# An RWKV block on one core: intra-chunk pair products in 64-token instead of 32-token blocks, k^T v of two chunks issued together, and a planner that counts shape changes and table loads

## The chip, the cores and the metric

The kernel runs on one core of one Trainium2 chip. The metric is device time in microseconds, as a median of several runs. A core has five engines that matter here: TensorE (PE) multiplies matrices; VectorE (DVE), ScalarE (ACT) and GpSimd (POOL) work elementwise; SyncE (SP) issues transfers. They run side by side, each through its own queue in order, and meet by semaphores. SBUF is the on-chip memory; PSUM is where TensorE writes its products.

## The reference

The input `x` is (2 sequences, 4096 tokens, 256 channels), all float32. It goes through a normalisation modulated by a condition, two RWKV layers, a second modulated normalisation and a feed-forward network with FP4 rounding. What matters here is the recurrence `_wkv` in each layer's time mix, with 4 heads of 64 channels:

```python
def step(state, inp):
    rt, kt, vt, wt = inp
    kv = kt[..., :, None] * vt[..., None, :]
    out = jnp.einsum('bhk,bhkv->bhv', rt, state + u[None, :, :, None] * kv)
    return (state * wt[..., None] + kv, out)
...
x = x + _time_mix(_ln(x, p['ln1_w']), p)
x = x + _channel_mix(_ln(x, p['ln2_w']), p)
```

`w` is a decay per channel and token. Within a chunk of tokens the recurrence can be written as products of pairs: token t receives from token s < t the value `v_s`, weighted by the sum over channels of `r_t * k_s * (decays between s and t)`; token t itself enters with the bonus `u`.

## The kernel before

Tokens go in tiles of 256 (`TT`), each two chunks of 128 (`C` = 2). A head pair fills 128 channels, so there are `J` = 2 pairs, and inside a pair `p` = 0, 1 selects the head. There are 16 tiles per sequence, hence 64 calls of `wkv` (2 sequences, 2 layers, 16 tiles).

**Order of the work.** The kernel writes generators ("streams"): a first-layer and a second-layer stream for each sequence, one for the feed-forward network, one that prepares its weights and one for the conditioning. The streams don't issue instructions themselves; they record them with `Plan`. Successive TensorE calls of one generator step form one `Op`. `Plan.run` is a list scheduler: it estimates for every recorded operation when it could start, from `weight` (the cost of an instruction), the free time of its engine and the ends of what it depends on (`after`), takes the operation that could start earliest, and emits it (`give_out`), which moves its engine's time on. So each engine's order is fixed when the kernel is built, by these estimates, and at run time each engine follows its order and waits on semaphores. All instructions recorded this way appear in the profile under one line, L248, where `give_out` calls them; they are told apart by the names of their tiles. Work tiles come from a stock of `SLOTS` = 36 tiles of 128 x 514 floats; a stream records no further while the stock is below its `least`.

**Inside `wkv`.** One call at a time holds `head_lock`. The pair weights of a chunk are built by levels l = 0 to 6. Level l handles pairs of tokens (s, t) whose highest differing bit is bit l. For l < 5 (`NLEV`) the kernel multiplies whole diagonal blocks of 32 tokens, four per chunk, `K[.., s0:s0+32]` against `R[.., s0:s0+32]`, for both chunks, both head pairs and both heads: 32 `matmul` calls of 64 rows x 32 columns with 32 moving columns. They go to `pa`, two PSUM banks (one for each head), at one of four column positions (`l % 4`). Level 5 multiplies the off-diagonal 32 x 32 blocks (two a chunk, 16 calls), level 6 the off-diagonal 64 x 64 block (one a chunk, 8 calls). After each level DVE multiplies the decays of that level into `r` and `k` (`upd`) and forms the products of decays (`nt`); the next level's products need `upd`.

Of a level's block only the entries of that level are valid. `copy_predicated` on DVE copies them with `masks[:, l]` from `pa` into `diag`; this is recorded after level 3 for levels 0 to 3, and after level 6 for level 4. Levels 5 and 6 are copied by ACT straight from `pa` into `attn` (128 x 128 pair weights per head, pair and chunk). Four ACT copies then move the 32-token blocks from `diag` to the diagonal of `attn`. Meanwhile `k` is transposed to `kt`.

Then, for each chunk: the outputs `po` = `r` S + `attn` v, then k^T v into `kv` (4 calls of 128 x 64), then on DVE the state update S = S * tot + kv. Chunk 1's outputs need the S that chunk 0 updated.

**The costs.** `weight` gives a TensorE call with up to 32 columns 19 ns, a transpose 110 ns, other calls (4n/2.4 + 6) ns, times 0.55 where two halves of the array can work side by side. Nothing is charged when TensorE's operand shape changes, nor when ACT loads another function table.

Of the kernel before, what the change touches and what calls it, by code (L numbers as in the profile page):

```python
# [8 lines left out]
F32 = mybir.dt.float32  # L9
BF16 = mybir.dt.bfloat16  # L10
I32 = mybir.dt.int32
AF = mybir.ActivationFunctionType
# [19 lines left out]
LEAST = (8, 5, 3)  # L32
RUSH = 1.0
SOON = 40.0
SLOTS = 36
STAGGER = (12, 60)
SLOTS2 = 4
TINY = 24
# [51 lines left out]


class Op:
    __slots__ = ("eng", "calls", "cost", "port", "wait", "ready", "next", "end", "banks", "tiles", "age", "late")

    def __init__(self, eng, age):
        self.eng, self.age = eng, age
        self.calls, self.banks, self.tiles, self.next = [], {}, set(), []
        self.cost = self.ready = self.end = 0.0
        self.port = False
        self.wait = 0  # L100


class Plan:
# [15 lines left out]
    SEEN = {"tensor": 55.0, "gpsimd": 80.0}  # L119
    SAME = {"vector": 34.0, "scalar": 25.0, "gpsimd": 80.0}  # L120

    def after(self, o, op):
        return o.end + (self.SAME.get(o.eng, 0.0) if o.eng == op.eng else self.LAT[o.eng] + self.SEEN.get(op.eng, 35.0))

    def __init__(self, nc, banks):
        self.nc, self.banks = nc, [(0.0, b) for b in banks]
        self.probe = banks[0]
        self.seen = {}
        self.held = {}
        self.free = {e: 0.0 for e in self.ENG}  # L130
        self.lock = {"vector": 0.0, "gpsimd": 0.0}
        self.cur = None
        self.count = 0
        for e in self.ENG:
            setattr(self, e, Recorder(self, e))
# [67 lines left out]
    def record(self, eng, fn, a, k):  # L203
        st = self.cur
        outs = [k["out"]] if "out" in k else [a[0]]
        ins = list(a[0 if "out" in k else 1:]) + [v for n, v in k.items() if n != "out"]
        ins = [v for v in ins if isinstance(v, (bass.AP, Later))]
        cost, port = weight(eng, fn, outs[0], ins)
        op = st.last if eng == "tensor" else None
        if op is None or op.next is None:  # L210
            self.count += 1
            op = Op(eng, self.count)
            op.late = st.late
            st.queue.append(op)
        st.last = op if eng == "tensor" else None
        op.calls.append((getattr(getattr(self.nc, eng), fn), a, k))
        op.cost += cost
        op.port = op.port or port
        for v in ins:
            if not is_dram(v):  # L220
                self.need(op, v, False)
        for v in outs:
            if not is_dram(v):
                self.need(op, v, True)

    def start(self, op, st):
# [7 lines left out]
            t = max(t, self.lock["gpsimd" if op.eng == "vector" else "vector"] - 100.0)  # L234
        return t

    def give_out(self, op, t):
        for b in op.banks:
            if b.real is None:
# [6 lines left out]

        for fn, a, k in op.calls:
            fn(*[real(v) for v in a], **{n: real(v) for n, v in k.items()})  # L248
        op.end = t + op.cost
        self.free[op.eng] = t + (60.0 if op.eng == "sync" else op.cost - self.LAP.get(op.eng, 0.0))  # L250
        if op.port:
            self.lock[op.eng] = op.end
        for b in op.banks:
# [62 lines left out]
        return lambda *a, **k: self.plan.record(self.eng, fn, a, k)  # L316


def is_dram(v):
    return isinstance(v, bass.AP) and v.name.endswith("_dram")  # L320


def weight(eng, fn, out, ins):
# [4 lines left out]

    n = max(v.free_size() for v in [out] + ins)
    if eng == "tensor":  # L330
        if fn == "transpose":
            return 110.0, False
        n = out.free_size()
        if n <= 32:
            return 19.0, False
        pair = (n == 64 and out.shape[0] == 64) or (ins[0].shape[0] <= 64 and out.shape[0] == P and n == TT)
        return (4 * n / 2.4 + 6) * (0.55 if pair else 1.0), False
    if eng == "sync":
        return 100.0, False
    wide = [v for v in ins if v.free_size() > 1]  # L340
# [17 lines left out]
def rwkv_adaln_fp4_kernel(ctx: ExitStack, tc: tile.TileContext, a: dict, out: bass.AP):  # L358
# [28 lines left out]

    masks = const.tile([P, NLEV, 32], I32, name="masks")  # L390
    with tc.tile_pool(name="mk", bufs=1) as mk:
        s_i = mk.tile([P, 32], I32, name="s_i")
        t_i = mk.tile([P, 32], I32, name="t_i")
        x_i = mk.tile([P, 32], I32, name="x_i")
        g_i = mk.tile([P, 32], I32, name="g_i")
        y_i = mk.tile([P, 32], I32, name="y_i")
        nc.gpsimd.iota(s_i, pattern=[[0, 32]], base=0, channel_multiplier=1)
        nc.gpsimd.iota(t_i, pattern=[[1, 32]], base=0, channel_multiplier=0)
        nc.vector.tensor_scalar(s_i, s_i, 31, None, ALU.bitwise_and)
# [190 lines left out]
    for i in range(L):  # L590
        for b in range(B):
            nc.gpsimd.memset(state[i][b], 0.0)
            for m in range(2):
                nc.gpsimd.memset(carry[i][b][m], 0.0)
    diag = keep.tile([P, 2, C, J, 32], F32, name="diag")
    attn = keep.tile([P, 2, C, J, P], F32, name="attn")
    nc.gpsimd.memset(diag, 0.0)
    nc.vector.memset(kv, 0.0)
# [143 lines left out]
    def wkv(i, b, rk_s, dec_s, v_s):  # L742
# [20 lines left out]
        for l in range(7):  # L763
            h = 1 << l
            R, K = (r0, k0) if l == 0 else (r, k)
            wid = 64 if l == 6 else 32
            col0 = (l % 4) * C * J * 32
            cols = slice(col0, col0 + C * J * wid)
            pv = pa[:, :, cols].rearrange("p a (c j t) -> p a c j t", c=C, j=J)

            if l < NLEV:
                at0 = [(q, q) for q in (0, 32, 64, 96)]
            else:
                at0 = [(0, 32), (64, 96)] if l == 5 else [(0, 64)]
            for c in range(C):
# [21 lines left out]
            pl.vector.tensor_tensor(nt, tv[:, :, 0], tv[:, :, 1], ALU.mult)  # L797
            tot = nt

            ready = {3: range(0, 4), 6: range(4, 7)}.get(l, ())  # L800
            for m in ready:
                mw = 64 if m == 6 else 32
                c0 = (m % 4) * C * J * 32
                mc = slice(c0, c0 + C * J * mw)
                if m < NLEV:
                    pl.vector.copy_predicated(
                        diag.rearrange("p a c j t -> p a (c j) t"),
                        masks[:, m, :].unsqueeze(1).unsqueeze(1).to_broadcast([P, 2, C * J, 32]),
                        pa[:, :, mc].rearrange("p a (n t) -> p a n t", t=32),
                    )  # L810
                else:
                    for s0, t0 in [(0, 32), (64, 96)] if m == 5 else [(0, 64)]:
                        pl.scalar.copy(
                            attn[s0 : s0 + mw].rearrange("p a c j t -> p a (c j) t")[:, :, :, t0 : t0 + mw],
                            pa[s0 : s0 + mw, :, mc].rearrange("p a (n t) -> p a n t", t=mw),
                        )
            yield
        give(dec_s)
        tot = tot.rearrange("p (c j) -> p c j", c=C)
        for q in range(4):  # L820
            qs = slice(32 * q, 32 * (q + 1))
            pl.scalar.copy(
                attn[qs].rearrange("p a c j t -> p (a c j) t")[:, :, qs],
                diag[qs].rearrange("p a c j t -> p (a c j) t"),
# [14 lines left out]
        n = C * H  # L839
        few = pl.take(tiny)  # L840
        rs = few[:, :n]
        for c in range(C):
            for j in range(J):
                mm(po[:, c, j * P : (j + 1) * P], r[:, c, j, :], S[:, j, :], True, False)
                for p in range(2):
                    hd = slice((2 * j + p) * HS, (2 * j + p + 1) * HS)
                    mm(po[:, c, hd], attn[:, p, c, j, :], v[:, c, hd], False, p == 1)

            for j in range(J):
                for p in range(2):  # L850
# [447 lines left out]
```

## Time and profile before

| what | value |
|---|---|
| median of 3 runs | 3298.43 us (3298.05 to 3305.83) |
| profiled execution | 3307.55 us |
| its span, first to last instruction | 3305.8 us |
| mean granted TensorE clock | 0.967 |
| TensorE busy | 3075.7 us, 93% |
| VectorE busy | 2396.8 us, 73% |
| ScalarE busy | 1628.8 us, 49% |
| GpSimd busy | 938.5 us, 28% |
| table loads on ScalarE | 133 of 1283 ns |

Rows of the profile read: line, engine, operation, tiles written <- tiles read, array shape and partitions x elements, count | busy us, mean ns of one | idle time of the engine before them and what ended it. A float32 `matmul` call appears as two MATMUL and two LDWEIGHTS instructions, so 32 calls are 64 rows. "64*32 64x32" is a product with 64 rows and 32 columns of weights and 32 moving columns. The ends of matmuls are modelled, and many overlap.

### The profile page before, as it was taken

The page shows a single profiled execution, that of the slowest core. Times are in us where ns is not written, and L with a number is a line of the kernel's source. Part 1 is how long each engine was busy: PE and PEld are TensorE (multiplying, and loading weights), DVE is VectorE, ACT ScalarE, POOL GpSimd, SP SyncE. Part 2 cuts the span into 40 slices and gives each one's busy share as a digit, 9 for nine tenths or more (in the row PEclk, how much of TensorE's full clock was granted, in tenths as well). Part 3 has the DMA queues.
Part 4 walks back from the last instruction along what each step waited for, and adds up shares of the span by engine and source line. Part 5 has one row for each costly group of instructions (what it writes and reads, how often), then busy time and mean ns, then how long its engine had stood idle before and what let it go on. Part 6 is the DMA issues. An engine that isn't in the chain of part 4 may idle for free. (4 is left out here: it accounts for less than half of the span.)

```text
span 3305.8 us, 88142 instructions
## 1 busy us (share of the span) xinstructions
PE 3075.7 (93%) x37948; PEld 2448.4 (74%) x37948; DVE 2396.8 (73%) x6146; ACT 1628.8 (49%) x3240; POOL 938.5 (28%) x857
## 2 busy tenths in 40 slices
PE   3899999999999999999999999999999999999965
PEld 1678778777777877777887777877777877877743
DVE  3777687777777687777777777778767787866764
ACT  1455455555555555555555555455554555444321
POOL 1233223233223233323233322333322233321200
PEclk8899999999999999999999999999999999998977
DMA  4000000000000000000000000000000000000000
GB/s 126 17 16 5 11 9 14 5 8 14 8 11 5 15 8 11 8 9 11 8 15 8 11 8 5 17 5 15 4 8 15 8 15 8 5 8 8 14 4 10
DMA packets 46856, 42.31 MB, mean 13 GB/s; under 512 B 13185, under 2 KB 44930, under 8 KB 46466
## 3 DMA queue, kind: packets, MB, share of 16 engines
q1 hardware_dynamic: 36962, 31.75, 3.2%
q8 instruction: 298, 4.88, 0.6%
q10 hardware_dynamic: 9504, 4.93, 0.5%
q14 instruction: 92, 0.75, 0.1%
HBM read 28.28 MB, written 8.39 MB: 11 GB/s over the span
## 5 line engine op out<-in xcount | busy, mean ns | idle before, releaser
L248 POOL TENSOR_TENSOR slot<-slot,slot 128x512 f32<-128x512 f32 x416 | 499.5, 1214 | 1016.4 <-DVE slot L248 614.9
L248 ACT ACTIVATE slot<-bank 128x512 f32<-128x512 f32 (+1 forms) x644 | 338.9, 531 | 753.3 <-PE bank L248 714.9
L248 POOL TENSOR_TENSOR tiny<-tiny,nhalf 128x2 f32<-128x2 f32 (+1 forms) x288 | 295.0, 1028 | 1018.2 <-DVE tiny L248 960.5
L248 DVE TENSOR_TENSOR slot<-slot,slot 128x512 f32<-128x512 f32 x512 | 381.6, 747 | 121.4 <-PE pa L248 88.7
L248 PE MATMUL bank<-slot,cWk 128*128 128x256 f32 x1536 | 375.8, 391 | 14.5 <-DVE slot L248 12.3
L248 PE MATMUL bank<-cWv,slot 128*128 128x256 f32 x1536 | 345.4, 381 | 0.0
L248 PEld LDWEIGHTS pa<-slot 64*32 64x32 f32 x19456 | 226.0, 109 | 156.3 <-DVE slot L248 56.5
L248 PEld LDWEIGHTS bank<-slot,cWk 128*128 128x128 f32 x1536 | 289.4, 194 | 62.1 <-DVE slot L248 15.7
L248 PEld LDWEIGHTS bank<-cWv,slot 128*128 128x128 f32 x1536 | 289.4, 190 | 41.0 <-ACT slot L248 0.7
L248 ACT ACTIVATE slot<-bank,vec 128x256 f32<-128x256 f32 x512 | 234.4, 496 | 166.6 <-PE bank L248 159.4
L248 PE MATMUL pa<-slot 64*32 64x32 f32 x19456 | 271.6, 203 | 38.0 <-DVE slot L248 24.0
L248 DVE SCALAR_TENSOR_TENSOR slot<-bank,vec,slot 128x256 f32<-128x256 f32 x640 | 275.1, 474 | 29.5 <-PE bank L248 28.1
L248 DVE TENSOR_TENSOR slot<-slot,bank 128x512 f32<-128x512 f32 x192 | 131.3, 684 | 200.8 <-PE bank L248 173.1
L248 POOL TENSOR_TENSOR slot<-slot 128x512 f32<-128x512 f32 x128 | 143.2, 1120 | 322.8 <-ACT slot L248 253.0
L248 DVE TENSOR_TENSOR long<-long,bank 128x352 f32<-128x352 f32 x256 | 131.7, 515 | 113.9 <-ACT long L248 91.7
L248 ACT ACTIVATE slot<-slot,tiny 128x256 f32<-128x256 f32 x256 | 141.8, 593 | 135.7 <-DVE tiny L248 114.7
L248 PE MATMUL bank<-ident,slot 128*128 128x128 f32 x1152 | 181.3, 286 | 23.9 <-ACT slot L248 18.1
L248 ACT ACT_TABLE_LOAD x133 | 170.6, 1283 | 46.6 <-DMA td<-in_L_attn_td_w_dram 38.3
L248 PE MATMUL bank<-wd,long 128*128 128x256 f32 x768 | 192.3, 403 | 1.2 <-ACT long L248 1.2
L248 PE MATMUL bank<-wg,slot 128*128 128x352 f32 x512 | 180.0, 474 | 4.6 <-ACT slot L248 4.4
L248 PEld LDWEIGHTS bank<-ident,slot 128*128 128x128 f32 x1152 | 136.6, 144 | 61.7 <-ACT slot L248 24.0
L248 DVE SCALAR_TENSOR_TENSOR slot<-slot,vec,slot 128x256 f32<-128x256 f32 x384 | 177.6, 493 | 5.8 <-POOL slot L248 5.7
(112 smaller groups left out, 5837.0 us busy)
## 6 DMA issues: line engine op xcount, KB each, us to landing
slot<-in_L_attn_x_dram SPq DMA_DIRECT2D x63, 256.0 KB, 2.7
out_dram<-slot SPq DMA_DIRECT2D x32, 256.0 KB, 2.1
cWv<-in_L_attn_cWv_dram SPq DMA_DIRECT2D x1, 768.0 KB, 9.4
cWk<-in_L_attn_cWk_dram ACTq DMA_DIRECT2D x1, 768.0 KB, 8.1
slot<-in_L_wmod_dram SPq DMA_DIRECT2D x3, 256.0 KB, 7.3
slot<-in_L_wmod_dram ACTq DMA_DIRECT2D x3, 256.0 KB, 6.5
cWk<-in_L_attn_cWk_dram SPq DMA_DIRECT2D x1, 768.0 KB, 4.8
cWv<-in_L_attn_cWv_dram ACTq DMA_DIRECT2D x1, 768.0 KB, 8.4
```

The costliest lines, as they stand in the source:

```text
L248: fn(*[real(v) for v in a], **{n: real(v) for n, v in k.items()})
```

## The change

Pair products. `masks` and `diag` become 64 wide. For levels 0 to 4 the kernel multiplies two diagonal blocks of 64 tokens a chunk in place of four of 32: 16 calls of 64 x 64 with 64 moving columns in place of 32 calls of 64 x 32 with 32. Two such levels fill `pa` (`l % 2`), so the masked copies are recorded in pairs, after levels 1, 3 and 5. Level 5 keeps its 16 calls of 32 x 32 blocks; ACT now copies it into `diag`, and two ACT copies of 64-token blocks move `diag` to `attn`.

k^T v. The 8 calls of both chunks are recorded together, in a generator step of their own, ahead of both chunks' outputs.

Planner. `form` names the array shape of a TensorE operation, and the table of an ACT activation where it is a sigmoid or an exponential. `give_out` adds `TURN` (94 ns, 1283 ns) to an operation's end when the form differs from the last of that engine; `start`, by which operations are chosen, doesn't use it. The TensorE costs in `weight` are set anew. `SLOTS` goes from 36 to 35.

```diff
-SLOTS = 36
+SLOTS = 35
...
+    TURN = {"tensor": 94.0, "scalar": 1283.0}
...
         op.calls.append((getattr(getattr(self.nc, eng), fn), a, k))
+        f = form(eng, fn, outs[0], ins, a)
+        if f is not None:
+            if op.forms and op.forms[-1] != f:
+                op.cost += self.TURN[eng]
+            op.forms.append(f)
         op.cost += cost
...
+    def turn(self, op):
+
+        return self.TURN[op.eng] if op.forms and op.forms[0] != self.form[op.eng] else 0.0
...
-        op.end = t + op.cost
-        self.free[op.eng] = t + (60.0 if op.eng == "sync" else op.cost - self.LAP.get(op.eng, 0.0))
+        op.end = t + op.cost + self.turn(op)
+        if op.forms:
+            self.form[op.eng] = op.forms[-1]
+        self.free[op.eng] = t + (60.0 if op.eng == "sync" else op.end - t - self.LAP.get(op.eng, 0.0))
...
+def form(eng, fn, out, ins, a):
+    if eng == "tensor":
+        return (ins[0].shape[0], P if fn == "transpose" else out.shape[0])
+    if eng == "scalar" and fn == "activation" and a[2] in (AF.Sigmoid, AF.Exp):
+        return a[2]
...
     if eng == "tensor":
+        n, rows, cols = out.free_size(), ins[0].shape[0], out.shape[0]
         if fn == "transpose":
             return 110.0, False
-        n = out.free_size()
-        if n <= 32:
-            return 19.0, False
-        pair = (n == 64 and out.shape[0] == 64) or (ins[0].shape[0] <= 64 and out.shape[0] == P and n == TT)
-        return (4 * n / 2.4 + 6) * (0.55 if pair else 1.0), False
+        if rows == P and cols == P:
+            return max(4 * n / 2.4 + 6, 195.0 if n == 64 else 265.0 if n == P else 0.0), False
+        if n <= 64:
+            return {(64, 32): 22.0, (64, 64): 66.0, (P, 64): 70.0}.get((rows, cols), 2 * n), False
+        return 0.55 * (4 * n / 2.4 + 6), False
...
-    masks = const.tile([P, NLEV, 32], I32, name="masks")
+    masks = const.tile([P, NLEV, 64], I32, name="masks")
...
-    diag = keep.tile([P, 2, C, J, 32], F32, name="diag")
+    diag = keep.tile([P, 2, C, J, 64], F32, name="diag")
...
-            wid = 64 if l == 6 else 32
-            col0 = (l % 4) * C * J * 32
+            wid = 32 if l == 5 else 64
+            col0 = 0 if l == 6 else (l % 2) * C * J * 64
...
-                at0 = [(q, q) for q in (0, 32, 64, 96)]
+                at0 = [(0, 0), (64, 64)]
...
-            ready = {3: range(0, 4), 6: range(4, 7)}.get(l, ())
-            for m in ready:
-                mw = 64 if m == 6 else 32
-                c0 = (m % 4) * C * J * 32
+            for m in {1: (0, 1), 3: (2, 3), 5: (4, 5), 6: (6,)}.get(l, ()):
+                mw = 32 if m == 5 else 64
+                c0 = 0 if m == 6 else (m % 2) * C * J * 64
...
-                        masks[:, m, :].unsqueeze(1).unsqueeze(1).to_broadcast([P, 2, C * J, 32]),
-                        pa[:, :, mc].rearrange("p a (n t) -> p a n t", t=32),
+                        masks[:, m, :].unsqueeze(1).unsqueeze(1).to_broadcast([P, 2, C * J, 64]),
+                        pa[:, :, mc].rearrange("p a (n t) -> p a n t", t=64),
...
-                    for s0, t0 in [(0, 32), (64, 96)] if m == 5 else [(0, 64)]:
+                    dst = diag if m == 5 else attn
+                    for s0, t0 in [(0, 32), (64, 32)] if m == 5 else [(0, 64)]:
                         pl.scalar.copy(
-                            attn[s0 : s0 + mw].rearrange("p a c j t -> p a (c j) t")[:, :, :, t0 : t0 + mw],
+                            dst[s0 : s0 + mw].rearrange("p a c j t -> p a (c j) t")[:, :, :, t0 : t0 + mw],
...
-        for q in range(4):
-            qs = slice(32 * q, 32 * (q + 1))
+        for q in range(2):
+            qs = slice(64 * q, 64 * (q + 1))
...
+        for c in range(C):
+            for j in range(J):
+                for p in range(2):
+                    hd = slice((2 * j + p) * HS, (2 * j + p + 1) * HS)
+                    mm(kv[p * HS : (p + 1) * HS, c, j, p * HS : (p + 1) * HS], kt[:, c, hd], v[:, c, hd], True, True)
+        yield
         for c in range(C):
             for j in range(J):
                 mm(po[:, c, j * P : (j + 1) * P], r[:, c, j, :], S[:, j, :], True, False)
...
-            for j in range(J):
-                for p in range(2):
-                    hd = slice((2 * j + p) * HS, (2 * j + p + 1) * HS)
-                    mm(kv[p * HS : (p + 1) * HS, c, j, p * HS : (p + 1) * HS], kt[:, c, hd], v[:, c, hd], True, True)
```

More of the change, by code (lines that the diff above doesn't have):

```diff
@@ L92 @@
 class Op:
-    __slots__ = ("eng", "calls", "cost", "port", "wait", "ready", "next", "end", "banks", "tiles", "age", "late")
+    __slots__ = ("eng", "calls", "cost", "port", "wait", "ready", "next", "end", "banks", "tiles", "age", "late", "forms")
     def __init__(self, eng, age):
@@ L98, in __init__ @@
         self.cost = self.ready = self.end = 0.0
+        self.forms = []
         self.port = False
@@ L131, in __init__ @@
         self.lock = {"vector": 0.0, "gpsimd": 0.0}
+        self.form = {"tensor": None, "scalar": None}
         self.cur = None
@@ L386, in rwkv_adaln_fp4_kernel @@
     nc.gpsimd.memset(nhalf, -0.5)
-    masks = const.tile([P, NLEV, 32], I32, name="masks")
+    masks = const.tile([P, NLEV, 64], I32, name="masks")
     with tc.tile_pool(name="mk", bufs=1) as mk:
[L392 to L399, printed above, removed]
+        s_i = mk.tile([P, 64], I32, name="s_i")
+        t_i = mk.tile([P, 64], I32, name="t_i")
+        x_i = mk.tile([P, 64], I32, name="x_i")
+        g_i = mk.tile([P, 64], I32, name="g_i")
+        y_i = mk.tile([P, 64], I32, name="y_i")
+        nc.gpsimd.iota(s_i, pattern=[[0, 64]], base=0, channel_multiplier=1)
+        nc.gpsimd.iota(t_i, pattern=[[1, 64]], base=0, channel_multiplier=0)
+        nc.vector.tensor_scalar(s_i, s_i, 63, None, ALU.bitwise_and)
         nc.vector.tensor_tensor(x_i, s_i, t_i, ALU.bitwise_xor)
```

## The prediction

> **What bounds the kernel.** I read the page first, then busy time by stretch, then the waits of TensorE (PE), then the groups by shape, and last PE's timeline inside one `wkv`. The page's engine line and the stretch from 200 to 3100 us:
>
> ```profile
> PE 3075.7 (93%) x37948; PEld 2448.4 (74%) x37948; DVE 2396.8 (73%) x6146; ACT 1628.8 (49%) x3240; POOL 938.5 (28%) x857
> PEclk8899999999999999999999999999999999998977
> ...
> sum 2900.00, PE 2812.22 PEld 2251.78 DVE 2162.87 ACT 1518.98 POOL 877.38; mean PE 401.75 PEld 321.68 DVE 308.98 ACT 217.00 POOL 125.34
> ```
>
> In those 2900 us PE is busy for 2812.2 and idle for 87.8 us, at a granted clock of 0.97 to 1.00. VectorE (DVE) has 75% and ScalarE (ACT) 52% there. So PE sets the pace: a nanosecond of PE work saved in the middle comes off the time, and work added to DVE or ACT costs only as far as it makes PE wait. PE's own waits in that stretch:
>
> ```profile
> PE pa L248 <- DVE slot L248: 19.1, 27, 2.1
> PE bank L248 <- ACT slot L248: 16.1, 25, 2.0
> PE bank L248 <- DVE slot L248: 14.5, 21, 2.7
> PE bank L248 <- POOL slot L248: 11.4, 12, 2.5
> PE bank L248 <- DVE long L248: 5.6, 9, 1.9
> PE pa L248 <- ACT slot L248: 5.5, 10, 1.5
> PE pa L248 <- DVE diag L248: 3.0, 4, 1.5
> ```
>
> The first number is us in total. DVE ends some 45 us of them (the rows above and one of 2.5 for the carry), ACT some 24. Matmul ends are modelled, so a group's busy time says little about small overlapping matmuls; I use the time from the start of one burst to the start of the next. PE's timeline (start, us, what, count of instructions; each float32 `matmul` call is two):
>
> ```profile
> 1544.51 1.03 PE L248 MATMUL bank<-slot,td 128*128 128x256 f32 x4
> 1545.47 0.76 PE L248 MATMUL pa<-slot,slot 64*32 64x32 f32 x64
> ...
> 1547.73 0.76 PE L248 MATMUL pa<-slot 64*32 64x32 f32 x64 [0.45 <-DVE slot L248]
> 1548.42 1.99 PE L248 MATMUL bank<-slot,Wr 128*128 128x256 f32 x8
> ...
> 1560.79 0.46 PE L248 MATMUL pa<-slot 64*32 64x32 f32 x32
> 1561.17 1.45 PE L248 MATMUL bank<-wu,slot 128*128 128x352 f32 x4
> 1562.74 0.68 PE L248 MATMUL pa<-slot 64*64 64x64 f32 x16
> 1563.35 0.48 PE L248 MATMUL bank<-slot,w2b 32*128 32x256 f32 x2
> ...
> 1569.08 0.45 PE L248 MATMUL kv<-slot,slot 128*64 128x64 f32 x8
> 1569.46 1.99 PE L248 MATMUL bank<-slot,Wg 128*128 128x256 f32 x8
> ```
>
> A level of today's pair products (64 instructions of 64x32) takes 1548.42 - 1547.73 = 0.69 us, 0.686 as the median over the bursts of 64. Level 5 (32 instructions) takes 0.385, level 6 (16 of 64x64) 0.612, and a burst of `kv` (8) 0.382. Where two 64x32 levels stand next to each other, the first takes 0.53; so about 0.155 of each lone level is filling and leaving, and 0.53/64 = 8.3 ns is one instruction. A change of shape costs PE about 0.093: eight 128x256 instructions with their like on both sides take 1.73 us, 0.216 each, and four would take 0.864, but they take 0.96 when a 64x32 burst follows (1545.47 - 1544.51).
>
> **Levels 0 to 4 as 64-token blocks.** Per level 64 instructions become 32, each with 64 columns of weights and 64 moving columns. No row has this with all four tiles in use; three rows bracket it. Level 6 uses two row tiles and one column tile: (612 - 155)/16 = 28.6 ns an instruction, 57 per tile. `kv` uses two column tiles and has the same: (382 - 155)/8 = 28.4. Level 5 uses two by two tiles with 32 columns: (385 - 155)/32 = 7.2 ns, 29 per tile, so all four do run at once. With four tiles the new level is 8 instructions per tile x 57 + 155 = **0.61 us**. The floor is the streaming itself: 216 ns for 256 columns is 54 for 64, and 8 x 54 + 155 = 0.587. The ceiling is two tiles at a time, 16 x 57 + 155 = 1.07. I take 0.612, since level 5 is the same tile pattern in the same order of calls. There are 64 `wkv` (2 layers, 2 sequences, 16 tiles) with 5 levels: 320 x (0.612 - 0.686) = **-23.7 us**, with ends -32 and +122.
>
> A rule that speaks against this: the Trainium skill, "TensorE: Matmul & The Clock Gate", section "Part 3: Packing small matmuls — row/col tiling", says that a weight load overlaps matmuls in flight only if its row group differs. Two column tiles of one row group would then go load, product, load, product: with 54 ns for each, the 16 instructions of a row group take 16 x 108 = 1.73 us, and the 320 levels would cost about +334 us. Level 6 contradicts it: 57 ns per instruction in a row group has room for one of the two, not both, so loads do hide behind products of their own row group. I follow the row.
>
> **k^T v of both chunks together.** Today there are two bursts of 8 per `wkv`, each after the `attn` products. Each costs 0.093 to turn and 0.382, the turn out of it included: 0.95 in all. One burst of 16 costs 0.093 + 0.382 + 8 x 0.0284 = 0.70. Saved: 0.24 x 64 = **-15.4 us** (if only the fill and one turn are saved -9.5). It now waits for `kt` alone and stands ahead of the outputs, so the state update of chunk 0 no longer has products of k^T v ahead of it; the second chunk's outputs are ready sooner. Behind other streams' work that is worth nothing more.
>
> **DVE: `copy_predicated` of twice the width.** The copies grow from 256 to 512 elements:
>
> ```profile
> L248 DVE COPY_PREDICATED diag<-masks,pa 128x256 f32<-128x256 int32 x320 | 139.9, 437 | 23.4 <-ACT attn L248 13.0 <-PE pa L248 7.1 <-ACT slot L248 1.3
> L248 DVE TENSOR_TENSOR slot<-slot,bank 128x512 f32<-128x512 f32 x192 | 131.3, 684 | 200.8 <-PE bank L248 173.1 <-ACT slot L248 20.4 <-issue 6.1
> L248 DVE TENSOR_TENSOR slot<-bank,gb 128x256 f32<-128x256 f32 x64 | 26.9, 420 | 58.2 <-PE bank L248 57.9
> ```
>
> The two tensor_tensor rows that read PSUM give 684 - 420 = 264 ns for 256 more elements, so a copy takes 437 + 264 = 0.70 us, and 320 of them add **84 us of DVE time**. The skill's "TensorEngine Tiling (Array Packing)", section "PSUM Bottleneck", warns of just this: tiling speeds up the products and not what empties PSUM. If DVE were the bound, the whole 84 us would be on the path and the change would lose. Here DVE rises in the middle from 75% to about 78%. What covers it is PE's work for the other streams. Queueing gives an estimate: waits grow like busy over idle, 2.9 to 3.5, a fifth of the 45 us that PE waits for DVE: **+9 us**. Without the cover it is +84.
>
> **Half as many levels fit into `pa`.** Two levels of 64 columns fill what four of 32 did. Today levels 4, 5 and 6 may wait for a copy out of `pa`, afterwards levels 2 to 6, three more per `wkv`. Behind a waiting level stand, in PE's queue, the other streams' products, which are what hides it. Today's three cost 3.0 us in all (the `diag` row of the waits). I take **+3 us**. If every new wait showed one whole copy, 192 x 0.7 = +134.
>
> **ACT.** Four copies of `diag` (402 ns each) become two of 64 partitions x 512. The nearest row, `attn<-pa 64x512`, has 572: 1.6 us become 1.1 per `wkv`, and ACT loses 30 us of work. The copies of level 5 into `diag` now come ahead of them. PE waits for `attn` only 2.3 us in all, so nothing is gained on the path.
>
> **The planner's costs.** They issue nothing; they only change orders. Until now a table load was free to it, though the page has 133 at 1283 ns, 171 us of ACT. It also priced an `attn` call at 113 ns, where the bursts show 2 x 112, and a shape change at nothing. That its order is late exactly where ACT loads a table is an inference. I take half of ACT's 24 us of PE waits: **-12 us**. Bounds: half of the 88 us of idle PE gained, or as much lost, since one order is exchanged for another, and since its new 66 ns a call puts a 64-token level at 16 x 66 + 94 = 1.15 us, almost twice my figure. One slot fewer of 36, the wider masks and memsets at the start (the first slice of 82.6 us has PE at 3 tenths, waiting for loads): nothing, at worst +10.
>
> **Sum.** -23.7 - 15.4 + 9 + 3 - 12 = -39 us. The profiled execution took 3307.55 us, 1.75 around its span of 3305.8; it becomes 3268.5. That execution stands 0.28% above the median of the runs, 3298.43, so the median becomes **3259 us**.
>
> **Rivals.** (1) *Only two tiles run at once* when they are 64 columns wide. Place: the 320 levels. Price: 1.07 instead of 0.612, 382 ns more than today at 0.686, so the sum is +122 - 15 + 9 + 3 - 12 = +107: 3405 us. It decides the sign once a level takes over 0.73 us: the other terms come to -15.4, and 15.4/320 = 0.048 above 0.686 eats them. For it: no row shows four such tiles, and the new planner prices a call as if so. Against it: level 5, and `kv` and level 6 each at full rate. (2) *PE stalls where it had cover*: DVE's longer copies with `pa` half as deep put 0.2 us more wait in front of each of 192 levels, 38 us: no change, 3297. For it: the largest row of PE's waits is already `pa <- DVE slot`. Against it: that row is only 27 waits of 320 levels. (3) *The better-informed order fills PE*: half of the 88 us of idle go on top of the products' 39, without the DVE terms: 3215 us. For it: the costs corrected are large (171 us of tables, 1368 changes of shape by my count over the bursts, 128 us). Against it: turn costs enter end times, not the choice, so turns are counted and not avoided.
>
> **Numbers.** The forecast has 0.58, rival 1 0.09, rival 2 0.13, rival 3 0.20. A difference under 0.3% (10 us) can't be told from none here. Faster: the forecast, rival 3 and a little of rival 2, 0.82; same 0.05; slower 0.13. The forecast's own range is 3235 to 3285. The 8-in-10 range takes in rival 3 and the centre of rival 2 and leaves out rival 1 and the far ends: 3205 to 3300.
>
> **What will show it.** A lone 64x64 burst of 32 instructions should be followed after 0.61 us (1.07: rival 1). `kv` should have 64 bursts of 16, 0.61 us each without the turn in. `copy_predicated` should read 0.70 us, DVE about 2480 us busy, ACT's copies of `diag` 128 at 0.57. Idle PE between 200 and 3100 should stay near 88 us; well above it is rival 2, well below it rival 3. The forecast is wrong if PE's idle moves by more than 40 us or the level is off by 0.1.

## The result, and the profile after

The changed kernel takes 3283.4 us in the median, the one before 3298.2 in the same comparison: a ratio of 0.9957, 95% interval 0.9935 to 0.9979. That is 15 us less where 39 were forecast. The profiled execution, the fastest of its runs, took 3275.78 us with a span of 3274.0. The profiled execution of the kernel before had a granted clock of 0.967, while its 20 runs beside the first experiments have 0.973 in the median, so some of its busy time is clock and not work. From the page of the changed kernel (all recorded instructions now stand under L262), the engines and the masked copies:

```profile
PE 3030.3 (93%) x27708; PEld 2401.6 (73%) x27708; DVE 2487.9 (76%) x6146; ACT 1602.6 (49%) x3120; POOL 946.3 (29%) x857
...
L262 DVE COPY_PREDICATED diag<-masks,pa 128x512 f32<-128x512 int32 x320 | 231.4, 723 | 10.7 <-PE pa L262 9.2
```

Its busy time from 200 to 3100 us, and TensorE's waits in that stretch (us in total, times, longest):

```profile
sum 2900.00, PE 2779.17 PEld 2212.42 DVE 2256.38 ACT 1485.03 POOL 879.15; mean PE 2779.17 PEld 2212.42 DVE 2256.38 ACT 1485.03 POOL 879.15
```

```profile
PE pa L262 <- DVE slot L262: 20.6, 33, 2.5
PE pa L262 <- DVE diag L262: 17.9, 22, 3.1
PE bank L262 <- POOL slot L262: 17.1, 23, 3.0
PE bank L262 <- DVE long L262: 16.6, 11, 6.2
PE bank L262 <- ACT slot L262: 15.9, 33, 1.9
PE bank L262 <- DVE slot L262: 13.0, 19, 1.9
PE pa L262 <- ACT diag L262: 8.4, 14, 1.7
```

TensorE is busy for 45 us less over the span (up to 26 of them because stretches at half clock cost 86 us in place of 112, summed over the clock's records), but it is idle for 2900 - 2779.2 = 120.8 us in the stretch where it was idle for 87.8. The waits name where: `pa <- DVE diag`, a level that waits for a masked copy, grew from 3.0 to 17.9, and a new row says that levels wait for ACT's copies of level 5 into `diag`. `bank <- DVE long` grew too, from 5.6 to 16.6, away from the levels.

TensorE's timeline in one `wkv` of the changed kernel:

```profile
1529.13 0.69 PE L262 MATMUL pa<-slot,slot 64*64 64x64 f32 x32
1529.78 0.69 PE L262 MATMUL pa<-slot 64*64 64x64 f32 x32
1530.40 1.99 PE L262 MATMUL bank<-Wo,slot 128*128 128x256 f32 x8
...
1534.71 0.69 PE L262 MATMUL pa<-slot 64*64 64x64 f32 x32
1535.34 1.99 PE L262 MATMUL bank<-cWr,slot 128*128 128x256 f32 x8
...
1552.83 0.68 PE L262 MATMUL pa<-slot 64*64 64x64 f32 x16
1553.44 1.99 PE L262 MATMUL bank<-slot,w 128*128 128x256 f32 x8
...
1557.09 0.69 PE L262 MATMUL kv<-slot,slot 128*64 128x64 f32 x16
1557.70 0.48 PE L262 MATMUL bank<-slot,w2b 32*128 32x256 f32 x2
```

A level of 32 instructions on four tiles takes 0.62 to 0.65 us from its start to the next (median over the lone bursts 0.625), hardly more than level 6 with its 16 on two (0.61). `kv` has 64 bursts of 16 with a median of 0.615. So a lone level costs what the forecast said. The loss is in what stands around the levels.

### The profile page after: what moved, and what is told of

Read it like the earlier page. It is cut to its first block, busy times and chain, and to the rows that moved or that the text cites. A ratio compares the mean times of both kernels' runs of the same rounds, so it can differ in the third digit from the quotient of the medians.

```text
span 3274.0 us, 67459 instructions
## 1 busy us (share of the span) xinstructions
PE 3030.3 (93%) x27708; PEld 2401.6 (73%) x27708; DVE 2487.9 (76%) x6146; ACT 1602.6 (49%) x3120; POOL 946.3 (29%) x857
## 5 line engine op out<-in xcount | busy, mean ns | idle before, releaser
L262 POOL TENSOR_TENSOR slot<-slot,slot 128x512 f32<-128x512 f32 x416 | 505.0, 1228 | 932.3 <-DVE slot L262 600.7
L262 ACT ACTIVATE slot<-bank 128x512 f32<-128x512 f32 (+1 forms) x644 | 339.5, 531 | 688.0 <-PE bank L262 654.7
L262 POOL TENSOR_TENSOR tiny<-tiny,nhalf 128x2 f32<-128x2 f32 (+1 forms) x288 | 295.6, 1029 | 1046.7 <-DVE tiny L262 977.5
L262 DVE TENSOR_TENSOR slot<-slot,slot 128x512 f32<-128x512 f32 x512 | 374.2, 734 | 70.7 <-PE pa L262 58.8
L262 PE MATMUL bank<-slot,cWk 128*128 128x256 f32 x1536 | 373.5, 390 | 3.2 <-DVE slot L262 3.1
L262 PE MATMUL bank<-cWv,slot 128*128 128x256 f32 x1536 | 344.9, 381 | 0.5 <-ACT slot L262 0.4
L262 PEld LDWEIGHTS pa<-slot 64*64 64x64 f32 x11264 | 203.7, 132 | 177.6 <-DVE slot L262 59.4
L262 PEld LDWEIGHTS bank<-slot,cWk 128*128 128x128 f32 x1536 | 289.3, 193 | 51.6 <-DVE slot L262 4.2
L262 PEld LDWEIGHTS bank<-cWv,slot 128*128 128x128 f32 x1536 | 288.7, 190 | 41.6 <-ACT slot L262 1.0
L262 PE MATMUL pa<-slot 64*64 64x64 f32 x11264 | 253.3, 221 | 56.7 <-DVE slot L262 23.2
L262 ACT ACTIVATE slot<-bank,vec 128x256 f32<-128x256 f32 x512 | 237.5, 497 | 135.1 <-PE bank L262 127.5
L262 DVE SCALAR_TENSOR_TENSOR slot<-bank,vec,slot 128x256 f32<-128x256 f32 x640 | 273.8, 473 | 23.1 <-PE bank L262 20.8
L262 DVE TENSOR_TENSOR slot<-slot,bank 128x512 f32<-128x512 f32 x192 | 131.1, 683 | 200.2 <-PE bank L262 177.3
L262 POOL TENSOR_TENSOR slot<-slot 128x512 f32<-128x512 f32 x128 | 143.9, 1127 | 339.3 <-ACT slot L262 250.0
L262 DVE COPY_PREDICATED diag<-masks,pa 128x512 f32<-128x512 int32 x320 | 231.4, 723 | 10.7 <-PE pa L262 9.2
L262 PE MATMUL bank<-ident,slot 128*128 128x128 f32 x1152 | 179.8, 282 | 36.4 <-ACT slot L262 22.7
L262 ACT ACTIVATE slot<-slot,tiny 128x256 f32<-128x256 f32 x256 | 142.0, 595 | 136.8 <-DVE tiny L262 116.8
L262 DVE TENSOR_TENSOR long<-long,bank 128x352 f32<-128x352 f32 x256 | 131.5, 514 | 94.4 <-ACT long L262 70.2
L262 ACT ACT_TABLE_LOAD x141 | 180.9, 1283 | 43.7 <-DMA td<-in_L_attn_td_w_dram 36.5
L262 DVE SCALAR_TENSOR_TENSOR slot<-slot,vec,slot 128x256 f32<-128x256 f32 x384 | 181.4, 508 | 19.7 <-POOL slot L262 19.7
L262 PE MATMUL bank<-wd,long 128*128 128x256 f32 x768 | 192.2, 403 | 0.9 <-ACT long L262 0.9
L262 PEld LDWEIGHTS bank<-ident,slot 128*128 128x128 f32 x1152 | 134.3, 143 | 76.5 <-ACT slot L262 31.6
```

## The experiments

The letters A, B and C stand for three theories of the new idle time; the first expectation states them. D, in the later runs, is that the times differ because each edit deals the planner another order. Idle time below is TensorE's between 200 and 3100 us. All ratios are against the kernel before, which ran beside each of them.

### One part at a time

**planner_only**: the kernel before with `form`, `TURN` and the new costs.

```diff
+    TURN = {"tensor": 94.0, "scalar": 1283.0}
...
+        op.end = t + op.cost + self.turn(op)
...
+            return {(64, 32): 22.0, (64, 64): 66.0, (P, 64): 70.0}.get((rows, cols), 2 * n), False
```

> The kernel before with the planner's part alone (form, TURN, the new TensorE costs; 36 slots, 32-token levels, k^T v after the outputs). Three theories for the 33 us of new idle time of TensorE between 200 and 3100 us in the changed kernel (120.8 against 87.8). A, the copies out of pa: two levels instead of four fit, so levels 2, 4 and 6 wait for copies. B, the load: DVE has 91 us more to do. C, the plan: the new costs give a worse order. A and B expect no loss here: ratio 0.996 to 1.000, TensorE idle 75 to 90 us in that stretch. C expects 1.005 to 1.010 and 105 to 120 us idle.

Measured: 3203.4 us, 0.9725 (0.9709 to 0.9741), idle 61 us. Neither C's loss nor the small gain of A and B: the planner alone gains 92 us, six times what the whole change gains. Its stretch and its waits:

```profile
sum 2900.00, PE 2838.66 PEld 2282.98 DVE 2237.27 ACT 1515.97 POOL 881.93; mean PE 2838.66 PEld 2282.98 DVE 2237.27 ACT 1515.97 POOL 881.93
```

```profile
PE bank L262 <- DVE long L262: 9.6, 5, 7.3
PE bank L262 <- POOL slot L262: 8.0, 12, 2.6
PE pa L262 <- DVE slot L262: 7.6, 9, 1.9
PE bank L262 <- ACT slot L262: 6.8, 15, 1.4
```

With the very instructions of the kernel before, the waits for DVE in `pa` fall from 19.1 to 7.6 us and those for ACT in `bank` from 16.1 to 6.8. The granted clock follows: 0.981 or 0.982 in all four runs, against 0.970 to 0.977 in the runs of the kernel before beside them. The last section shows what the clock does after a pause.

**kv_only**: the kernel before with k^T v of both chunks recorded ahead of the outputs.

```diff
+        for c in range(C):
+            for j in range(J):
+                for p in range(2):
...
+                    mm(kv[p * HS : (p + 1) * HS, c, j, p * HS : (p + 1) * HS], kt[:, c, hd], v[:, c, hd], True, True)
+        yield
         for c in range(C):
             for j in range(J):
                 mm(po[:, c, j * P : (j + 1) * P], r[:, c, j, :], S[:, j, :], True, False)
```

> The kernel before with k^T v of both chunks ahead of the outputs and nothing else. By the bursts 64 x 0.24 us = 15.4 us of TensorE work go: all theories expect TensorE busy about 15 us lower, its idle time near 88 us, ratio 0.995 (3282 us). A rival says that the gain is eaten because k^T v now stands ahead of outputs that someone waits for: ratio 1.000.

Measured: 3283.9 us, 0.9968 (0.9956 to 0.998). TensorE is busy for 3051.1 us, 25 less, but idle for 113 us in place of 88, so 11 us are left of it in the time. The work went, and part of it came back as waiting. (Of the 25, only some 15 can be k^T v; the profiled execution of the kernel before also had the lower clock, 0.967 against 0.973.)

**no_planner**: the blocks and k^T v, old planner, 35 slots; `LEAST` lets the second layer's stream stop recording at 6 free tiles in place of 5.

```diff
-    TURN = {"tensor": 94.0, "scalar": 1283.0}
...
-LEAST = (8, 5, 3)
+LEAST = (8, 6, 3)
```

> The changed kernel with the old planner (old costs, no TURN, 35 slots; the second layer's stream stops recording at 6 free tiles instead of 5). A and B expect the idle time to stay: TensorE idle 110 to 130 us between 200 and 3100 us, ratio 0.994 to 0.998. C expects idle near 88 us and a ratio of 0.985 to 0.988.

Measured: 3301.8 us, 1.0021 (1.0009 to 1.0032), idle 147 us. The idle time is there without the new planner. C falls. Against kv_only the blocks cost 0.0053 here, 17 us.

**price33**: the changed kernel with the right price for a block level.

```diff
-            return {(64, 32): 22.0, (64, 64): 66.0, (P, 64): 70.0}.get((rows, cols), 2 * n), False
+            return {(64, 32): 22.0, (64, 64): PAIR[0], (P, 64): 70.0}.get((rows, cols), 2 * n), False
...
+            PAIR[0] = 33.0 if l < NLEV else 66.0
```

> The changed kernel, where the planner prices a call of levels 0 to 4 at 33 ns and one of level 6 at 66 (the trace has 625 ns for 16 calls and 612 for 8). Nothing that runs differs but the order. If the wrong price made the idle time (C): idle 85 to 100 us, ratio 0.985 to 0.989. A and B expect the changed kernel's values: idle 110 to 130 us, ratio 0.994 to 0.997.

Measured: 3273.7 us, 0.9935 (0.9919 to 0.9951), idle 116 us: 0.002 better than the changed kernel and no nearer to the 0.985 of C.

**planner_kv**: everything but the blocks (32-token levels, 36 slots), as a diff to the changed kernel.

```diff
-SLOTS = 35
+SLOTS = 36
...
-                at0 = [(0, 0), (64, 64)]
+                at0 = [(q, q) for q in (0, 32, 64, 96)]
```

> The planner's part and k^T v ahead, with 32-token levels and 36 slots: the changed kernel without its 64-token blocks. The planner alone gave a ratio of 0.9725 and k^T v alone 0.9968. If they add, this is 0.969 to 0.970 (3195 us), and the blocks, taken with this planner, cost 0.026 (87 us), all of it idle time of TensorE, since the blocks have 22 us less TensorE work. If k^T v and the planner are what don't go together, this is 0.985 to 0.996.

Measured: 3255.4 us, 0.9867 (0.9848 to 0.9886), idle 97 us. The parts don't add: 0.9725 and 0.9968 make 0.9867. Against it the blocks cost 0.009. But it left open whether k^T v or merely this order is the cause; see the last group.

### The places in pa

**pk_two_places**: planner_kv with the changed kernel's places and pairs of copies, at the old width.

```diff
-            col0 = (l % 4) * C * J * 32
+            col0 = 0 if l == 6 else (l % 2) * C * J * 64
-            ready = {3: range(0, 4), 6: range(4, 7)}.get(l, ())
+            ready = {1: (0, 1), 3: (2, 3), 5: (4, 5), 6: (6,)}.get(l, ())
```

> As planner_kv, with 32-token levels and copies of 256 elements, but only two places in pa in place of four, and the copies recorded in pairs after levels 1, 3 and 5 as in the changed kernel. A (levels 2, 4 and 6 wait for copies) expects most of the loss here: ratio 0.983 to 0.992, TensorE idle over 100 us between 200 and 3100 us. B (the load of the wider copies on DVE) expects nothing: 0.967 to 0.972, idle 60 to 70 us.

Measured: 3222.2 us, 0.9761 (0.9742 to 0.9779), idle 76 us. It lies between the two expectations, below planner_kv (0.9867). Two places don't cost anything here, and `pa <- DVE diag` stays short:

```profile
PE pa L262 <- DVE diag L262: 4.3, 8, 1.3
```

A falls as the main cause.

**free_price**: price33 with the waits for copies loosened. `region` reckons columns of `pa` within a bank, and the copies move ahead of the decays.

```diff
+        if ap.name.startswith("pa"):
+            lo = lo % 512
+            hi = lo + 1 + sum((c - 1) * t for t, c in ap.ap[1:] if t < 512)
...
-            for m in {1: (0, 1), 3: (2, 3), 5: (4, 5), 6: (6,)}.get(l, ()):
+            for m in {1: (0,), 2: (1,), 3: (2,), 4: (3,), 5: (4,), 6: (5, 6)}.get(l, ()):
```

> As price33 (0.9935), but the planner tells the column places of pa apart, and each masked copy is recorded one level later and ahead of that level's decays, so a level waits only for the copy of the level two before it, and level 6 no longer for ACT's copies of level 5. DVE's work is the same. A expects most of the idle time to go: ratio 0.968 to 0.978. B expects it to stay: 0.988 to 0.995.

Measured: 3323.4 us, 1.0072 (1.0056 to 1.0088), idle 141 us. It missed both expectations and went the other way from A. The copy of a level now stands on DVE in front of every update of decays, which the next level needs; that this is why was not tested apart.

### DVE's work, in an order that stays

The planner deals a new order whenever a cost changes. So the next runs change the work at the moment of issue, in `give_out`, behind the planner's back. All engines keep their order, instruction for instruction.

**half_copy** came first and still went through the planner: every other column of a copy, its cost reckoned from 256 elements.

```diff
-                        diag.rearrange("p a c j t -> p a (c j) t"),
+                        diag.rearrange("p a c j t -> p a (c j) t")[:, :, :, 0:64:2],
```

> The changed kernel with every masked copy moving only every other column, 256 elements in place of 512; the other pair weights are left out, so its values are not the reference's, and only its time is read. The waits for copies stay, DVE loses about 91 us of work. The planner reckons the shorter copies. A expects little: ratio 0.988 to 0.996. B expects the loss to go: 0.968 to 0.976, TensorE idle 60 to 80 us between 200 and 3100 us.

Measured: 3349.4 us, 1.0158 (1.0138 to 1.0178), idle 186 us. Its groups by shape say why it does not test B:

```profile
L262 DVE COPY_PREDICATED diag<-masks,pa 128x256 f32<-128x256 int32 x320 | 231.2, 723 | 7.9 <-PE pa L262 6.2
```

Half the elements with a step of two take 723 ns, as all 512 do. No DVE work was saved, while the planner reckoned with 417 ns. What it has instead is a copy priced 0.3 us too low, 320 times, and 66 us more than the changed kernel; how much of that is the price and how much the luck of another order was not tried apart.

**half_fixed**: the changed kernel in its own order, with only the first 32 columns of each block copied; the pair weights of the other columns are left out.

```diff
+        if op.eng == "vector" and op.calls[0][0].__name__ == "copy_predicated":
+            fn, a, k = op.calls[0]
+            op.calls = [(fn, tuple(v[:, :, :, 0:32] for v in a), k)]
```

> The changed kernel in its own order, instruction for instruction, but each masked copy moves only the first 32 columns of a block (256 elements in one piece of 32, not every other column); the other pair weights are left out, so only its time is read. DVE loses 320 x 0.28 = 90 us of work and every wait for a copy gets shorter. B and A expect the loss against planner_kv to go: ratio 0.975 to 0.987. D expects 0.990 to 0.996.

Measured: 3233.2 us, 0.9797 (0.9783 to 0.981), idle 100 us. Its copies and its waits:

```profile
L265 DVE COPY_PREDICATED diag<-masks,pa 128x256 f32<-128x256 int32 x320 | 138.9, 434 | 10.0 <-PE pa L265 8.5
...
PE bank L265 <- DVE long L265: 16.5, 11, 6.2
...
PE pa L265 <- DVE slot L265: 13.6, 21, 2.2
PE pa L265 <- ACT diag L265: 6.4, 7, 2.1
PE pa L265 <- DVE diag L265: 5.8, 5, 2.0
```

`pa <- DVE diag` falls from 17.9 to 5.8 us; `bank <- DVE long` stays at 16.5, so that growth isn't the copies'. The 320 x 0.289 = 92 us of DVE work were worth 0.9957 - 0.9797 = 0.016, **53 us** of the time, in a kernel whose DVE is idle a quarter of the time. A and B both expected this, D did not. Between the two profiled spans (3274.0 and 3227.5 us) TensorE's idle time falls by 26 us, and the busy time of the very same instructions by 21: its stretches at half clock cost 70 us in place of 86.

**copy_twice**: planner_only in its own order, each masked copy issued twice.

```diff
+        if op.eng == "vector" and op.calls[0][0].__name__ == "copy_predicated":
+            op.calls = op.calls * 2
```

> planner_only (0.9725) with each masked copy issued twice in a row, without the planner knowing: the order of everything else is the same, and DVE has 320 x 0.44 = 140 us more to do, at the places where the changed kernel's copies grew. B (load on DVE) expects a loss well beyond the 84 us of the wider copies scaled by queueing, 40 to 100 us: ratio 0.985 to 1.003. A fourth theory, D, holds that DVE's load matters little and that the times differ because each edit deals the greedy planner another order: it expects 0.973 to 0.979.

Measured: 3347.5 us, 1.0147 (1.0131 to 1.0163), idle 138 us. Against planner_only 0.0422, **139 us for 140 us of DVE work**: one for one, more than B expected, and far from D. Its waits have one row that stands out:

```profile
PE pa L264 <- DVE diag L264: 63.0, 47, 4.2
PE pa L264 <- DVE slot L264: 13.5, 20, 2.7
```

The place isn't quite that of the changed kernel's growth: planner_only records the copies of levels 0 to 3 together after level 3, so the added work stands in one lump, and all of these waits fall on level 4 (68.6 us over the whole span). In the changed kernel the copies stand in pairs. So the direct price of its own longer copies is half_fixed's.

**stats_twice**: the same amount of DVE work in the layer norms.

```diff
+        if op.eng == "vector" and op.calls[0][0].__name__ == "bn_stats":
+            self.stats = getattr(self, "stats", 0) + 1
+            if self.stats % 4:
+                op.calls = op.calls * 2
```

> planner_only in its own order, with 336 of the 448 bn_stats (0.41 us each) issued twice without the planner knowing: 138 us more for DVE, as much as in copy_twice (ratio 1.0147), but in the layer norms of other streams, not between levels of pair products. If DVE's load as such sets the time, the ratio is again near 1.010 to 1.017. If it is the place, behind which the next level of products waits, it is 0.975 to 0.990.

Measured: 3296.0 us, 0.9995 (0.9984 to 1.0007), between the two expectations. 138 us of DVE work away from the levels cost 0.0270, **89 us**. So about two thirds of copy_twice's price come in this other place too, and a third goes with the place between two levels; other places were not tried. Here the waits are spread. First stats_twice, then planner_only, whose first row stands above as 7.6:

```profile
PE pa L266 <- DVE slot L266: 28.1, 38, 2.9
PE pa L266 <- DVE diag L266: 13.4, 14, 3.2
```

```profile
PE pa L262 <- DVE diag L262: 4.6, 6, 2.3
```

The levels wait for DVE although no work was added among them: their updates and copies come later in DVE's queue.

### What in the planner gains, and how much an order alone moves

**costs_only**, **tables_only** and **costs_turns** each take parts of the planner's edit: the TensorE costs alone; `TURN` for tables alone with the old costs; costs and `TURN` for shapes with tables free. As diffs to planner_only, first tables_only, then costs_turns (costs_only has no `TURN` at all):

```diff
-    TURN = {"tensor": 94.0, "scalar": 1283.0}
+    TURN = {"tensor": 0.0, "scalar": 1283.0}
...
-            return max(4 * n / 2.4 + 6, 195.0 if n == 64 else 265.0 if n == P else 0.0), False
```

```diff
-    TURN = {"tensor": 94.0, "scalar": 1283.0}
+    TURN = {"tensor": 94.0, "scalar": 0.0}
```

> The kernel before with the new TensorE costs in weight alone (no TURN). Both the planner's gain (0.9725) and its parts are open. If the products' costs (attn 113 to 195 ns a call, S 219 to 265, kv 62 to 70) are what was wrong, 0.975 to 0.985; if the table loads are, 0.995 to 1.002.

Measured: 1.0117 (1.009 to 1.0144).

> The kernel before with TURN counting ACT's table loads (1283 ns), nothing for changes of TensorE's shape and the old costs. If table loads are the planner's gain, 0.975 to 0.985, and TensorE waits less for ACT; if not, 0.995 to 1.002.

Measured: 0.9942 (0.9924 to 0.9961).

> The kernel before with the new TensorE costs and TURN for changes of shape (94 ns), but table loads free: the planner's part without tables. If tables carry the gain, 0.990 to 1.000; if TensorE's costs carry it, 0.970 to 0.978.

Measured: 1.0077 (1.0054 to 1.01). No part carries the gain by itself. With the new TensorE costs and tables free the kernel is slower than before; adding the tables to that moves it from 1.0077 to 0.9725. TensorE's waits for ACT show it. First costs_turns, then planner_only:

```profile
PE bank L262 <- ACT slot L262: 22.8, 30, 4.2
PE pa L262 <- ACT slot L262: 15.1, 20, 3.3
```

```profile
PE bank L262 <- ACT slot L262: 6.8, 15, 1.4
...
PE pa L262 <- ACT slot L262: 0.8, 1, 0.8
```

The loads themselves hardly change (125 against 127, 1283 ns each): they are not avoided, they are allowed for.

**before_42**, **planner_42**, **planner_kv_42** and **after_42** shift the window within which the planner picks by age, and nothing else.

```diff
-SOON = 40.0
+SOON = 42.0
```

> The kernel before with SOON at 42. The distance from 1.000 is the spread that an order alone gives the old planner: D expects 0.005 to 0.015 to either side.

> planner_only (0.9725) with SOON at 42 in place of 40: the same instructions in another order. If the planner's part is a real gain, 0.970 to 0.980. If 0.9725 is one lucky order among such as costs_turns (1.0077) and tables_only (0.9942), 0.985 to 1.005.

> planner_kv (0.9867) with SOON at 42: the same instructions in another order. If k^T v ahead truly goes ill with the planner, it stays at 0.985 to 0.989. D expects another time; where planner_kv was an unlucky order, 0.969 to 0.980.

> The changed kernel with the planner's window SOON at 42 ns in place of 40: the same instructions in another order, no work added or removed. A, B and C expect no change: 0.994 to 0.998. D expects another time, away from 0.9957 by 0.005 or more to either side.

Measured, as ratios to the kernel before:

| | SOON 40 | SOON 42 |
|---|---|---|
| before | 1 | 1.0064 (1.0044 to 1.0083) |
| planner alone | 0.9725 | 0.9798 (0.9782 to 0.9815) |
| planner and k^T v | 0.9867 | 0.9800 (0.9785 to 0.9814) |
| changed kernel | 0.9957 | 0.9989 (0.9981 to 0.9997) |

An order alone moves the time by 0.003 to 0.007, 11 to 24 us: as much as the whole result. planner_42 fits a real gain, as its expectation put it, and planner_kv_42 an unlucky order in planner_kv; after_42 moved by less than D expected and out of the range of A, B and C. The steps that keep their sign in both columns are the planner, -0.0275 and -0.0266, and the blocks (with one slot fewer), +0.0090 and +0.0189. k^T v with this planner, +0.0142 and +0.0002, can't be told from the luck of an order. planner_only is the fastest that ran, 3203 us, well ahead of both kernels.

## Why the prediction was wrong

The sign was right and the time lies in the range (3205 to 3300), but the gain is 15 us where 39 stood. That the time came so near is in part luck: the blocks lose where a gain was forecast, and the planner gains more than its term and hides a part of that. How much each part is worth depends on the order in which they are added (ratios times 3298 us; the blocks with one slot fewer):

| us | k^T v | blocks | planner |
|---|---|---|---|
| forecast | -15 | -23.7 + 9 + 3 = -12 | -12 |
| planner first, SOON 40 | +47 | +30 | -91 |
| planner first, SOON 42 | +1 | +62 | -88 |
| planner last: kv_only, no_planner, changed kernel | -11 | +17 | -21 |

**Right.** A lone level, forecast at 0.612 us, takes 0.625. Four tiles of 64 columns do run at once, where the rule that the prediction quotes from the Trainium skill's "TensorE: Matmul & The Clock Gate", "Part 3: Packing small matmuls — row/col tiling", would have made it 1.73. `kv` is one burst of 0.615. The copy takes 723 ns against 700, ACT's copies of `diag` 614 against 572, DVE is busy for 2488 us against 2480. Rival 1 is out.

**Wrong: "+9 us" for DVE's longer copies.** This is the step that failed, and with it the blocks' gain: they lose in every row of the table. It let waits grow like busy over idle, as if DVE could use its idle quarter whenever it liked. Taking 92 us out of the copies of the changed kernel at an unchanged order gave **53 us** back. Up to 16 us of that are TensorE work at half clock, which the prediction left out. The warning of the Trainium skill's "TensorEngine Tiling (Array Packing)", "PSUM Bottleneck", that tiling speeds up TensorE and not what empties PSUM, was set aside for want of a full DVE. It names no size; the prediction's own price for the case, the whole 84 us on the path, came nearer to the 53 than the 9 did. The reason that I draw from copy_twice and stats_twice is that both engines follow fixed orders and take turns waiting for each other, so DVE's idle time lies where it has nothing it may do; that is argued from the prices, and not shown by a run of its own. Idle PE rose by 33 us, to 121: towards rival 2, though short of the 40 that were set as a sign.

**Mis-sized: "-23.7 us" for the levels.** Timed from burst to burst without the waits, the pair products sum to 283 us in planner_kv and 270 in the changed kernel, 292 in kv_only and 278 in no_planner, 285 in planner_kv_42 and 268 in after_42: -13 to -17. Medians of lone bursts give 320 x (0.625 - 0.686) = -19.5; why the sums fall short of that was not looked into.

**Mis-sized: "-12 us" for the planner.** Alone on the kernel before it gains about 89 us (the mean of the two columns times 3298), as the last step 21, which an order's luck could also make. The mechanism named, table loads that nobody had allowed for, is part of it (38 us of waits for ACT slots fall to 8 between costs_turns and planner_only), but I took half of one engine's waits as its worth. Fewer waits of every kind and less time at half clock go with the rest. Why so little of it is left in the changed kernel stays open.

**"-15.4 us" for k^T v** is right as work and not as time: -11 with the old planner and nothing that can be told with the new one.

**"+3 us" for pa's two places** was not refuted: pk_two_places lost nothing. Which levels wait was told wrong, though: levels 2 to 6 are two more than levels 4 to 6, not three, and by a count over the bursts of the changed kernel the waits for copies fall on levels 2 (6.5 us) and 4 (12.7), and on level 6 for ACT's copies of level 5 (8.4); before, on level 4 alone (5.6). In half_fixed, with the same two places, levels 2 and 4 wait for 1.1 and 5.0: they are long because the copies are.

Two readings were a little off without moving the sum: where two 64x32 levels adjoin, the first takes 0.546 us or more in the trace and not 0.53, and k^T v's 0.95 less 0.70 make -16 and not -15.4.

The account of the blocks closes within the luck of an order: -13 to -17 us of products and +53 us of copies make +36 to +40; the table has +17, +30 and +62. What one slot fewer costs, and ACT's copy of level 5 into `diag`, were not tried apart. Rival 2, stalls where there was cover, had the right mechanism and a price of 38 us. Rival 3, the better-informed order, had the right sign; its 44 us stand against 91 for the planner alone and 21 for it as the last step. Both came true at once.

## What to carry to other kernels

In a kernel whose engines follow fixed, interlocked orders, an engine that is 75% busy need not have a free quarter: find what its work costs by doubling an operation, or shrinking it, at an unchanged order, before trading work from the busiest engine to it. This list scheduler gained more from better costs for two engines at once (TensorE's and ACT's table loads together, 89 us on the kernel before) than from either alone, which made it slower or hardly faster. And what a part gains alone need not be what it gains beside the others (21 us). Before a difference under 1% is given a cause, a neutral nudge to the planner shows how much of it is the order.

## What was not expected of the hardware

A masked copy of every other column (256 elements, a step of two) takes 723 ns, just what 512 adjacent columns take, while 256 in runs of 32 take 434 to 440.

And idle time costs clock. A pause of TensorE in the kernel before (stretch in us, its length, busy us of each engine with instructions, granted clock, DMA share, GB/s):

```profile
794.23:797.65 3.42, 1.44 (x39) 0.93 (x37) 1.12 (x4) 3.37 (x7) 1.04 (x1) 1.00 0.02 5
797.65:807.89 10.24, 10.24 (x43) 6.59 (x44) 5.59 (x13) 6.32 (x12) 2.14 (x2) 0.50 0.01 2
807.89:811.30 3.41, 3.41 (x26) 2.68 (x25) 2.42 (x8) 0.38 (x1) 1.09 (x1) 1.00 0.00 0
```

TensorE is busy for only 1.44 of 3.42 us, and then has half the clock for 10.24. In that stretch a level 6 takes 1.05 us from its start to the next burst, against 0.612. By the clock's records all 20 stretches at half clock between 100 and 3100 us begin so: in the 3.4 us before each, TensorE was idle for 0.96 to 2.5 us. planner_only has 9 there, each after 1.3 to 2.6 us idle. With the same instructions, its TensorE is idle for 55 us less over the span than in the profiled execution of the kernel before, and loses 50 us less to half clock (62 against 112, summed over the clock's records); part of this is that execution's low clock (0.967, against 0.973 in the median of the others).
